# Two fused network layers on one core: Vector takes over some transposes, and the last tile is added and stored behind the branch that repeats the attention

## The chip, the cores and the metric

The kernel runs on one core of a Trainium2 chip. The metric is device time in microseconds (us). Three runs of the kernel before gave 2710.21, 2710.99 and 2712.02 us; the median is 2710.99 us. Engines are named as in the profile: PE is TensorE, with PEld its weight loads; DVE is VectorE, ACT is ScalarE, POOL is GpSimd, SP is the engine that issues every DMA here.

## The reference, cut to what matters

The input x is 2 x 56 x 56 x 384 (6272 tokens of 384 channels) in float32. Two layers follow one another.

```python
# layer 0
h = neighborhood_attention(layer_norm(x, ln1_g, ln1_b))   # 12 heads of 32, window 7 x 7
x = x + h                                                  # h: softmax(q k + rpb) v @ w_proj + b_proj
x = x + gelu(layer_norm(x, ln2_g, ln2_b) @ w1 + b1) @ w2 + b2
# layer 1
p = layer_norm(x, n1_g, n1_b) @ w_in + b_in                # 384 -> 768
local = depthwise_conv_3x3(p)
mixed = 0.25 * (ema_lr + ema_rl + ema_tb + ema_bt)(local) + local
x = x + layer_norm(mixed, on_g, on_b) @ w_out + b_out      # 768 -> 384
x = x + gelu(layer_norm(x, n2_g, n2_b) @ w1 + b1) @ w2 + b2
```

Both MLPs have 1536 hidden channels. The softmax is computed without subtracting a maximum; sums that leave the range 1e-9 to 1e9 set a flag, and a branch at the end repeats everything in a slower, safe way. With the inputs of this case the flag is not set.

## The kernel before, in words

Tokens lie in tiles of 128, 49 in all. The work is written out by hand in the order in which each engine gets it; an engine runs its instructions in that order, and so does the DMA queue of SP.

**Attention** (main loop of `block_kernel`, L702 to L806). There are 14 groups of 8 image rows, 4 windows of 8 x 14 queries in each, and 3 units of 4 heads in each window: 168 units, one a step `s`. A unit's scores go to two PSUM tiles (L515), DVE adds the bias (L530), ACT takes the exponent (L536). The keys of a window lie in 2 or 3 chunks. `gathered` (L538) adds the chunks of a unit on DVE, with one addition for 2 chunks and two for 3 (L542, L544). `values` (L546) multiplies each chunk with the values (L552) and the added numerators with ones (L558), which gives the sums for the softmax. `END` (L701) is 12: in the last two groups the planner has less left to put between the units.

**The step from attention to the rest.** At step `s == NU` (168) the keys' memory is freed, and SP is given the loads of the last four tiles' residuals (L741) and then those of the first two groups of the next stage (L742), all behind the stores of that step (`store_all`, L704). A residual gets its bias on POOL (`add_bias`, L569), either when its counter `loaded` runs out or when the projection's result is added (L583). After the loop the projections that are still open are added (L808, L585), then the first group is measured and normalized (L810 to L813), and the remaining projections follow.

**MLP of layer 0 and entry to layer 1** (`passes`, first loop, L1341 to L1404). 13 groups of 2, 3, and eleven times 4 tiles. For a group, `hidden` (L1053) is called 12 times (3 matmuls and one GELU), and `tokens` (L1059) once for each tile (12 matmuls). Beside that the group before is normalized (L1357), turned to channels and put through `project_in` (L1384), and the next group is normalized and turned (L1390). Turning is `channels` (L1038), which calls `to_channels` (L245): for each of 3 channel blocks one PE transpose a tile into PSUM (L251), and one ACT instruction that takes the block to SBUF with gain and bias (L254). The object `beside` hands out the convolution and the scans, nearly all on DVE, in small steps between those calls; its jobs begin when the first band of rows has been through `project_in`, in the fourth group.

**Exit of layer 1 and its MLP** (second loop, L1428 to L1455). 13 groups of 4 (eleven times), 3 and 2 tiles. `load_mix` (L1233) loads the mixed channels, `measure` (L1246) turns each tile with 6 PE transposes into PSUM (L1251) so that DVE can take mean and variance, and `project_out` (L1266) multiplies by `w_out`. `measure_beside` (L1257) calls `measure` after every second `hidden`; the group `half_way`, the seventh, is measured two calls of `hidden` later than the others, since its mixed rows are the last that the scans finish. In the `tokens` part of a group, the next group is normalized (L1450), turned by `channels` (L1442), and each finished tile is added and stored (L1447, L1448). PSUM tiles named `y` come from a pool of two (L967).

**The end.** After the last tile's addition and store, every engine loads the flag into a register (L1464) and branches on it (L1465) over the repeated attention, whose instructions fill a block as long as the main one; behind the branch lie only the waits and barriers that end the program.

Of the kernel before, what the change touches and what calls it, by code (L numbers as in the profile page):

```python
# [42 lines left out]
P = 128  # L43
# [130 lines left out]
def block_kernel(ctx: ExitStack, tc: tile.TileContext, ins: dict, out: bass.AP):  # L174
# [328 lines left out]
    class Unit:  # L503
# [34 lines left out]
        def gathered(self):  # L538

            n, t = self.w.keys, lp.tile([P, 4, TT], F32, name="sum", bufs=2)  # L540
            self.sum = t
            nc.vector.tensor_tensor(t[:n], self.pts[:n, :, 0, :], self.pts[:n, :, 1, :], ALU.add)  # L542
            for c in range(2, self.m):
                nc.vector.tensor_tensor(t[:n], t[:n], self.pts[:n, :, c, :], ALU.add)  # L544

        def values(self):  # L546

            w, hg, n = self.w, self.hg, self.w.keys
            for c in range(self.m):
                for i in range(4):  # L550
                    h = 4 * hg + i
                    nc.tensor.matmul(  # L552
                        o[i * HD : (i + 1) * HD, hg, :],
                        lhsT=w.vt[:n, c, h * HD : (h + 1) * HD], rhs=self.pts[:n, i, c, :],
                        start=c == 0, stop=c == self.m - 1,
                    )
            for i in range(4):
                nc.tensor.matmul(  # L558
                    sums[i * HD : (i + 1) * HD, hg * TT : (hg + 1) * TT], lhsT=ones_hd[:n, :],
                    rhs=self.sum[:n, i, :], start=True, stop=True,  # L560
                )

    def load_residual(t, pool=lp, bufs=3):

        xrs[t] = pool.tile([P, C], F32, name="xr", bufs=bufs)
        nc.sync.dma_start(out=xrs[t], in_=xf[t * P : (t + 1) * P, :])
        loaded[t] = 4

# [133 lines left out]
    for s in range(NU + 4):  # L702
        n, k, hg, i = s // UG, s % UG, s % NC, s // NC
        store_all()  # L704
        while load:
# [28 lines left out]
        if s >= NU - UG - 4 and hg == 2 and w_parts:  # L734
            w_parts.pop(0)()
        if s == NU:
            kctx.close()
            xp = ctx.enter_context(tc.tile_pool(name="x", bufs=2, side="right", reuse_waits="tile"))
            tail_pool = actx.enter_context(tc.tile_pool(name="a_tail", bufs=1))
            for t in range(T2 // P - 4, T2 // P):  # L740
                load_residual(t, tail_pool, 4)  # L741
            xs = {g: load_group(x1f, groups[g], "xa") for g in range(2)}  # L742


# [56 lines left out]
        if n + 3 < ng:  # L801
# [3 lines left out]
            if k in (8, 9, 11):  # L805
                taking.append(channels_of(n + 3, (8, 9, 11).index(k), turning_bank))  # L806

    for take in taking:  # L808
        take()
    norm = norm_of(xs[0], groups[0][1], sm)  # L810
    norm.close(groups[0][1])
    norm.shift(groups[0][1])
# [10 lines left out]
    actx.close()  # L823

    def attention_again():

# [4 lines left out]
        ps_t = fctx.enter_context(tc.tile_pool(name="f_pst", bufs=2, space=PSUM))  # L831
        ps_s = fctx.enter_context(tc.tile_pool(name="f_pss", bufs=4, space=PSUM))
        ps_o = fctx.enter_context(tc.tile_pool(name="f_pso", bufs=1, space=PSUM))
# [3 lines left out]
        nc.sync.dma_start(out=wproj, in_=ins["L0_conv_w_proj"].rearrange("(c p) n -> p c n", p=P))  # L837
        shift = fp.tile([P, C], F32, name="shift")
        nc.sync.dma_start(out=shift, in_=b_proj.to_broadcast([P, C]))
# [119 lines left out]

    def passes(xs, xn, w1, w2, between=lambda psum: None):  # L960
        pctx = ExitStack()
# [4 lines left out]
        cp = pctx.enter_context(tc.tile_pool(name="conv", bufs=2))  # L966
        ps_y = pctx.enter_context(tc.tile_pool(name="psy", bufs=2, space=PSUM))  # L967
        ps_t = pctx.enter_context(tc.tile_pool(name="pst", bufs=3, space=PSUM))
# [13 lines left out]

        rows = wp.tile([P, 2, C], F32, name="rows")
        w_in = wp.tile([P, NC, INNER], F32, name="w_in")
        w_out = wp.tile([P, NI, C], F32, name="w_out")

        def load_row(i, name):
            r = ROWS[name]
            nc.sync.dma_start(
                out=rows[:, i, :], in_=ins["rows"][r : r + 1, :].to_broadcast([P, C])  # L990
            )

        def row(name):
# [9 lines left out]
        def prepare_w_out():  # L1003
# [7 lines left out]
            nc.vector.tensor_scalar_mul(pair[:, :, 1], og, 1.0 / INNER)  # L1011
            ps = ps_y.tile([P, C], F32, name="y")
            for c in range(NI):
# [24 lines left out]
        def channels(xn, n, g, b):  # L1038
            hT = io.tile([P, NC, MT], F32, name="hT")
            to_channels(ps_t, [xn[:, k, :] for k in range(n)], hT, NC, g, b)  # L1040
            return hT

        def columns(w, m, hT, n):

            ps = ps_m.tile([P, MT], F32, name="mm")
            for c in range(NC):
                nc.tensor.matmul(  # L1047
                    ps[:, : n * P], lhsT=w[:, c, m * P : (m + 1) * P], rhs=hT[:, c, : n * P],
                    start=c == 0, stop=c == NC - 1,
                )  # L1050
            return ps
# [7 lines left out]
        def tokens(lhs, w, k):  # L1059

            ps = ps_y.tile([P, C], F32, name="y")
            for m, t in enumerate(lhs):
                nc.tensor.matmul(  # L1063
                    ps, lhsT=t[:, k * P : (k + 1) * P], rhs=w[:, m, :],
                    start=m == 0, stop=m == len(lhs) - 1,
                )
            return ps
# [165 lines left out]
        def load_mix(g):  # L1233
            t0, n = dgroups[g]
            mx = io.tile([P, NI, MT], F32, name="mx")
            for b, at, here, n in images(t0, n * P):
                nc.sync.dma_start(
                    out=mx[:, :, here : here + n],
                    in_=mix_d[b][:, :, at : at + n].rearrange("m p t -> p m t"),
                )  # L1240
            x = load_group(x2_d, dgroups[g], "xa")
# [14 lines left out]

        def measure_beside(m, g, ahead, late=0):  # L1257

            n = dgroups[g][1]
            k = (m - late) // 2 - 1  # L1260
            if m % 2 == 1 and 0 <= k < n:
                measure(ahead[0], ahead[2], k)
            if m == min(10 + late, NHID - 1):
                ahead[2].close(n)
# [72 lines left out]

        def channels_n1(xn, n):
            return channels(xn, n, "L1_conv_n1_g", "L1_conv_n1_b")

        for g, (t0, n) in enumerate(groups):  # L1341
            hid = []
            preparing = prepare_w_out() if g == 1 else iter(())
            if g == last:
# [3 lines left out]
            for m in range(NHID):  # L1348
                next(preparing, None)
                if waiting is not None:  # L1350
# [5 lines left out]
                    if 2 <= m < 2 + groups[gw][1]:  # L1356
                        norm_w.apply_by_scalar(m - 2, x2w, xn_w)  # L1357
                    if m == (11 if g == 1 else 6):
                        store_x2(gw, x2w)
                    if m == NHID - 1:  # L1360
                        hT_w = channels_n1(xn_w, groups[gw][1])
                hid.append(hidden(w1, m, hT, n, "L0_conv_b1"))
# [18 lines left out]
            if g == 0:  # L1381
                between(ps_y)
            if waiting is not None:
                project_in(gw, hT_w)  # L1384
            if g == last:
                w1, w2_1, w_parts = weights(1)
                for part in w_parts[:3]:
                    part()
            if g < last:
                hT = channels(xn_next, n_next, "L0_conv_ln2_g", "L0_conv_ln2_b")  # L1390
            x2 = io.tile([P, NT, C], F32, name="xc")
# [21 lines left out]
        x3, norm = project_out(0, *ahead)  # L1413
        hT = channels_n1(xn, groups[g][1])

# [10 lines left out]
        project_in(g, hT, first_input)  # L1426
        hT = channels(first["xn"], dgroups[0][1], "L1_conv_n2_g", "L1_conv_n2_b")
        for g, (t0, n) in enumerate(dgroups):  # L1428
            hid = []
            for m in range(NHID):  # L1430
                hid.append(hidden(w1, m, hT, n, "L1_conv_b1"))
                if g < last:
                    measure_beside(m, g + 1, ahead, 2 if g + 1 == half_way else 0)
                beside.go(MLP_D)
# [5 lines left out]
            for k in range(n):  # L1440
                if k == n - 1 and g < last:
                    hT = channels(xn, dgroups[g + 1][1], "L1_conv_n2_g", "L1_conv_n2_b")  # L1442
                ps = tokens(hid, w2, k)
                o = res[:, k, :]
                if k == 0 and g < last:
                    norm.shift(dgroups[g + 1][1])
                nc.vector.tensor_tensor(o, ps, o, ALU.add)  # L1447
                nc.sync.dma_start(out=yout[t0 + k * P : t0 + (k + 1) * P, :], in_=o)  # L1448
                if k == n - 3 and g < last:
                    xn = normalized(norm, x3, dgroups[g + 1][1])  # L1450
                    add_row(x3, dgroups[g + 1][1], "b2_1")
                beside.go(ROW_D)
# [4 lines left out]

    def raise_flag(psum):
        ps = psum.tile([P, C], F32, name="y")
        nc.tensor.matmul(ps[:1, :1], lhsT=bad, rhs=ones[:, :1], start=True, stop=True)  # L1460
# [4 lines left out]
    with tc.If(again > 0):  # L1465
# [5 lines left out]
        with tc.tile_pool(name="small_again", bufs=1) as sm_again:  # L1471
# [3 lines left out]
            xn = normalized(norm, xs[0], groups[0][1])  # L1475
        passes(xs, xn, w1, w2)


# [67 lines left out]
```

## Time and profile before

| what | value |
|---|---|
| median of three runs | 2710.99 us |
| the profiled execution, its own time | 2709.48 us |
| its span, first to last instruction | 2707.7 us |
| mean granted TensorE clock | 0.996 |
| ACT busy | 897.7 us, 33% |
| POOL busy | 249.6 us, 9% |
| DMA, mean over the span | 110 GB/s |
| PE transposes of normalized tiles, L251 | x441, 55.4 us, 275 ns each |
| PE transposes of mixed tiles, L1251 | x294, 40.8 us, 276 ns each |
| matmuls of the softmax sums, L558 | x1344, 259 ns each |

The span is cut into 40 slices in one part of the page, with the busy share of each engine in tenths. A group of instructions has its busy time, the mean duration of one, and the idle time of its engine just before it with what ended that. The program's float32 matmuls stand in the trace twice each (two passes), its transposes once. Durations of neighbouring PE instructions overlap, so a sequence is shorter than the sum of its durations.

### The profile page before, as it was taken

How to read it: one execution, taken by the hardware profiler on the slowest of the kernel's cores; microseconds unless marked ns; L12 is line 12 of the kernel's file. 1: busy time of each engine (PE TensorE's matmuls, PEld its weight loads, DVE VectorE, ACT ScalarE, POOL GpSimd, SP SyncE). 2: the span in 40 equal slices, each digit the busy share in tenths (PEclk: the TensorE clock that was granted, in tenths of full speed). 3: DMA queues.
4: the chain of work that ended last, by engine and by line, in shares of the span. 5: the costliest groups of instructions: out<-in, count | busy, mean ns of one | idle time of the engine just before them, and what ended most of it. 6: DMA issues, size and time to landing. Idle time of an engine off the chain costs nothing. (4 is left out here: it accounts for less than half of the span.)

```text
span 2707.7 us, 36333 instructions
## 1 busy us (share of the span) xinstructions
PE 2659.7 (98%) x14975; PEld 1492.9 (55%) x14975; DVE 1679.7 (62%) x2560; ACT 897.7 (33%) x1447; POOL 249.6 (9%) x264
## 2 busy tenths in 40 slices
PE   8999999998899999999999999999999999999998
PEld 4666666655555555555554555555555455555565
DVE  3778877878320188688989888898888522221110
ACT  4555555554222332222344422321233211111111
POOL 1111111111211100000010000000100011110100
PEclk9999999999999999999999999999999999999999
DMA  6423454225410132232354544443354411011000
GB/s 213 133 88 104 150 174 149 77 75 167 135 47 27 64 115 79 104 118 98 120 199 183 206 143 141 164 136 117 142 188 171 153 47 44 12 41 35 30 12 16
DMA packets 131887, 298.91 MB, mean 110 GB/s; under 512 B 10646, under 2 KB 87552, under 8 KB 129408
## 3 DMA queue, kind: packets, MB, share of 16 engines
q1 hardware_dynamic: 131712, 296.50, 31.9%
q8 instruction: 119, 1.95, 0.3%
q14 instruction: 56, 0.46, 0.1%
HBM read 180.86 MB, written 115.61 MB: 109 GB/s over the span
## 5 line engine op out<-in xcount | busy, mean ns | idle before, releaser
L1047 PE MATMUL mm<-hT,w 128*128 128x512 f32 (+2 forms) x1872 | 776.1, 570 | 0.1
L1063 PE MATMUL y<-w,hid 128*128 128x384 f32 x2352 | 764.8, 486 | 0.0
L1063 PEld LDWEIGHTS y<-w,hid 128*128 128x128 f32 x2352 | 445.0, 190 | 305.3 <-issue 0.5
L1047 PEld LDWEIGHTS mm<-hT,w 128*128 128x128 f32 x1872 | 352.1, 191 | 372.8 <-issue 342.4
L1056 ACT ACTIVATE hid<-mm,chan 128x512 f32<-128x512 f32 (+2 forms) x312 | 206.3, 662 | 741.2 <-PE mm L1047 741.2
L1141 DVE SCALAR_TENSOR_TENSOR loc<-pt,taps,loc 128x990 f32<-128x990 f32 (+9 forms) x336 | 377.1, 1122 | 10.0 <-ACT loc L1123 1.7
L536 ACT ACTIVATE pts<-pts 119x448 f32<-119x448 f32 (+3 forms) x336 | 206.5, 642 | 187.9 <-DVE pts L530 187.9
L530 DVE TENSOR_TENSOR pts<-sc,bias 119x448 f32<-119x448 f32 (+3 forms) x336 | 220.8, 699 | 67.7 <-PE sc L515 66.7
L222 POOL TENSOR_TENSOR rs<-rs,mhalf 128x4 f32<-128x4 f32 (+4 forms) x67 | 87.2, 1302 | 1745.6 <-DVE rs L219 1704.1
L386 PE MATMUL ps<-hT,wqkv 128*128 128x448 f32 x504 | 211.9, 559 | 3.5 <-ACT vs L431 1.5
L1047 PE MATMUL mm<-hT,w_in 128*128 128x512 f32 (+2 forms) x468 | 191.7, 568 | 0.6 <-ACT hT L254 0.6
L1063 PE MATMUL y<-w_out,mx 128*128 128x384 f32 x588 | 191.8, 486 | 0.0
L1395 DVE TENSOR_TENSOR xc<-y,xa 128x384 f32<-128x384 f32 x49 | 27.3, 557 | 251.0 <-PE y L1063 250.5
L1447 DVE TENSOR_TENSOR xc<-y,xc 128x384 f32<-128x384 f32 x49 | 27.2, 555 | 218.2 <-PE y L1063 167.8
L1063 PEld LDWEIGHTS y<-w_out,mx 128*128 128x128 f32 x588 | 111.6, 190 | 79.8 <-issue 4.8
L240 ACT ACTIVATE xn<-xc,sh,rs 128x384 f32<-128x384 f32 x98 | 64.7, 698 | 269.3 <-DVE sh L233 269.1
L214 DVE BATCH_NORM_STATS2 st<-xi 128x6 f32<-128x384 f32 x98 | 50.3, 554 | 153.3 <-PE xi L1251 153.2
L1047 PEld LDWEIGHTS mm<-hT,w_in 128*128 128x128 f32 x468 | 88.7, 190 | 101.6 <-issue 91.8
L386 PEld LDWEIGHTS ps<-hT,wqkv 128*128 128x128 f32 x504 | 90.2, 191 | 84.4 <-issue 72.8
L254 ACT ACTIVATE hT<-tp,chan 128x512 f32<-128x512 f32 (+2 forms) x117 | 79.5, 751 | 165.1 <-PE tp L251 165.0
L515 PEld LDWEIGHTS sc<-qT,kT 32*100 32x100 f32 (+3 forms) x3168 | 90.9, 169 | 69.5 <-DVE pts L530 17.3
L515 PE MATMUL sc<-qT,kT 32*100 32x112 f32 (+3 forms) x3168 | 113.8, 270 | 9.0 <-DVE pts L530 8.4
(89 smaller groups left out, 2435.4 us busy)
## 6 DMA issues: line engine op xcount, KB each, us to landing
bias<-in_bias_t SPq DMA_DIRECT2D x16, 1344.0 KB
loc<-loc_d SPq DMA_DIRECT2D x24, 784.0 KB
mixed<-mix_d SPq DMA_DIRECT2D x24, 784.0 KB
mix_d<-mixed SPq DMA_DIRECT2D x24, 784.0 KB
xa<-x_d SPq DMA_DIRECT2D x22, 768.0 KB
p_d<-mx SPq DMA_DIRECT2D x10, 1536.0 KB
mx<-mix_d SPq DMA_DIRECT2D x10, 1536.0 KB
pt<-p_d SPq DMA_DIRECT2D x18, 560.0 KB
```

The lines of the kernel that those rows point to most:

```text
L214: nc.vector.bn_stats(st[:n, i, :], x)
L222: nc.gpsimd.tensor_tensor(rs, rs, mhalf[:n, :k], ALU.pow)
L240: nc.scalar.activation(out[:, k, :], x[:, k, :], AF.Identity, bias=self.sh[:n, k : k + 1], scale=self.rs[:n, k : k + 1],)
L254: nc.scalar.activation(dst[:, c, : len(xs) * n], tp, AF.Identity, bias=col(b, c), scale=col(g, c))
L386: nc.tensor.matmul(ps, lhsT=wqkv[:, c, m * P : (m + 1) * P], rhs=hT[:, c, half_of(n)], start=c == 0, stop=c == NC - 1,)
L515: nc.tensor.matmul(sc[i // 2][: w.keys, i % 2, (first + c) * TT : (first + c + 1) * TT], lhsT=kT[d, hg, w.keys_at + r * w.kc : w.keys_at + ...
L530: nc.vector.tensor_tensor(self.of(half), sc[half][:n, :, at].rearrange("p h (c q) -> p h c q", q=TT), self.w.bias[:n, 4 * self.hg + h : 4 ...
L536: nc.scalar.activation(self.of(half), self.of(half), AF.Exp)
L1047: nc.tensor.matmul(ps[:, : n * P], lhsT=w[:, c, m * P : (m + 1) * P], rhs=hT[:, c, : n * P], start=c == 0, stop=c == NC - 1,)
L1056: nc.scalar.activation(t[:, : n * P], ps[:, : n * P], AF.Gelu, bias=col(b1, m))
L1063: nc.tensor.matmul(ps, lhsT=t[:, k * P : (k + 1) * P], rhs=w[:, m, :], start=m == 0, stop=m == len(lhs) - 1,)
L1141: nc.vector.scalar_tensor_tensor(to, pt[:, lo + dy - self.top : hi + dy - self.top, xt : xt + n], self.tap(dy, dx), to, ALU.mult, ALU.add,)
```

## The change

It has seven parts.

1. In the last two attention groups DVE no longer adds the chunks; PE multiplies every chunk with ones and accumulates.
2. At step 168 the loads of the next stage's first groups are issued first, ahead of that step's stores, and the last residuals get their bias two steps later rather than at the end; the first group is measured before the open projections are added.
3. In the first loop of `passes`, from the second group until the scans begin, the turning is done by DVE in blocks of 32 x 32, and ACT applies gain and bias in SBUF.
4. In the second loop, from `half_way` on, the turning of the next group is done in the same way, its normalization is moved up to the first tile, and the tiles after `half_way` are measured from blocks that DVE turned.
5. The group `half_way` is loaded in steps of 128 tokens and measured at the same calls of `hidden` as the others.
6. One of the two PSUM tiles `y` becomes `y_end`, which outlives `passes`; the calls take the two in turn.
7. The last tile's residual is copied to `rows`; its addition to `y_end` and its store stand behind the branch.

```diff
         def gathered(self):
-            n, t = self.w.keys, lp.tile([P, 4, TT], F32, name="sum", bufs=2)
-            self.sum = t
+            n, self.parts = self.w.keys, [self.pts[:, :, c, :] for c in range(self.m)]
+            if self.w.n >= END:
+                return
+            t = lp.tile([P, 4, TT], F32, name="sum", bufs=2)
+            self.parts = [t]
...
-            for i in range(4):
-                nc.tensor.matmul(
-                    sums[i * HD : (i + 1) * HD, hg * TT : (hg + 1) * TT], lhsT=ones_hd[:n, :],
-                    rhs=self.sum[:n, i, :], start=True, stop=True,
-                )
+            for c, part in enumerate(self.parts):
+                for i in range(4):
+                    nc.tensor.matmul(
+                        sums[i * HD : (i + 1) * HD, hg * TT : (hg + 1) * TT], lhsT=ones_hd[:n, :],
+                        rhs=part[:n, i, :], start=c == 0, stop=c == len(self.parts) - 1,
+                    )
...
+        if s == NU:
+            kctx.close()
+            xp = ctx.enter_context(tc.tile_pool(name="x", bufs=2, side="right", reuse_waits="tile"))
+            tail_pool = actx.enter_context(tc.tile_pool(name="a_tail", bufs=1))
+            xs = {g: load_group(x1f, groups[g], "xa") for g in range(2)}
+            for t in range(T2 // P - 4, T2 // P):
+                load_residual(t, tail_pool, 4, 2)
         store_all()
...
-            for t in range(T2 // P - 4, T2 // P):
-                load_residual(t, tail_pool, 4)
-            xs = {g: load_group(x1f, groups[g], "xa") for g in range(2)}
...
+    norm = norm_of(xs[0], groups[0][1], sm)
+    norm.close(groups[0][1])
     for take in taking:
         take()
-    norm = norm_of(xs[0], groups[0][1], sm)
-    norm.close(groups[0][1])
     norm.shift(groups[0][1])
...
+        def turned(xn, k, hT):
+            for i in range(0, P, HD):
+                for j in range(0, P, HD):
+                    nc.vector.transpose(
+                        hT[j : j + HD, :, k * P + i : k * P + i + HD],
+                        xn[i : i + HD, k, :].rearrange("p (c q) -> p c q", c=NC)[:, :, j : j + HD],
+                    )
+        def scaled(hT, n, g, b):
+            for c in range(NC):
+                nc.scalar.activation(
+                    hT[:, c, : n * P], hT[:, c, : n * P], AF.Identity, bias=col(b, c),
+                    scale=col(g, c),
+                )
...
+            step = P if g == half_way else n * P
...
+        def measure_by_vector(mx, norm, k):
+            t = flat(half("turned", "work"))[:, : NI * P]
+            for i in range(0, P, HD):
+                for j in range(0, P, HD):
+                    nc.vector.transpose(
+                        t[j : j + HD].rearrange("p (m c) -> p m c", m=NI)[:, :, i : i + HD],
+                        mx[i : i + HD, :, k * P + j : k * P + j + HD],
+                    )
+            norm.add(k, [t[:, h * C : (h + 1) * C] for h in range(2)])
...
+            if g > half_way:
+                if m % 2 == 0 and m // 2 < n:
+                    measure_by_vector(ahead[0], ahead[2], m // 2)
+            elif m % 2 == 1 and 0 < m // 2 <= n:
+                measure(ahead[0], ahead[2], m // 2 - 1)
+            if m == 10:
                 ahead[2].close(n)
...
+            by_vector = 0 < g < last and not beside.busy()
...
+                    if by_vector and 3 <= m < 3 + groups[gw][1]:
+                        turned(xn_w, m - 3, hT_w)
...
+            if by_vector:
+                hT = io.tile([P, NC, MT], F32, name="hT")
+                for k in range(n_next):
+                    turned(xn_next, k, hT)
+                scaled(hT, n_next, *ln2)
...
+            by_vector = half_way <= g < last
...
+                if by_vector and 0 < k < n - 1:
+                    for q in range(2 * k - 2, min(2 * k, dgroups[g + 1][1])):
+                        turned(xn, q, hT)
+                elif by_vector and k == n - 1:
+                    scaled(hT, dgroups[g + 1][1], *n2)
...
+                if g == last and k == n - 1:
+                    assert ps is y_end and t0 + n * P == T2
+                    nc.vector.tensor_copy(rows[:, 1, :], o)
+                    break
                 nc.vector.tensor_tensor(o, ps, o, ALU.add)
...
         passes(xs, xn, w1, w2)
+    o = rows[:, 1, :]
+    nc.vector.tensor_tensor(o, y_end, o, ALU.add)
+    nc.sync.dma_start(out=yout[T2 - P :, :], in_=o)
```

## The prediction

> **What bounds the kernel now.** I read the busy shares first, then the waits of PE, then stretches of single stages.
>
> ```profile
> PE 2659.7 (98%) x14975; PEld 1492.9 (55%) x14975; DVE 1679.7 (62%) x2560; ACT 897.7 (33%) x1447; POOL 249.6 (9%) x264
> ...
> DVE  3778877878320188688989888898888522221110
> ```
>
> PE is busy for 98% of the span. DVE (one digit for each fortieth) is nearly idle in two places: around slices 11 to 13, before the scans begin, and from slice 31 to the end. What PE waits for, with total, times and longest, in us:
>
> ```profile
> PE sc L515 <- DVE pts L530: 8.4, 15, 1.5
> PE tp L251 <- DVE bad L820: 7.4, 1, 7.4
> PE xi L1251 <- DMA mx<-mix_d: 4.8, 1, 4.8
> ```
>
> Stretches (start:end, length, then PE, PEld, DVE, ACT, POOL busy, granted clock, DMA): one group of the second loop, the last two attention groups, and PE's restart after its 7.4 us wait.
>
> ```profile
> 2211.40:2292.70 81.30, 81.30 (x253) 44.74 (x252) 16.33 (x31) 12.86 (x19) 8.85 (x4) 1.00 0.12 39
> 616.00:652.00 36.00, 33.38 (x570) 21.23 (x562) 32.05 (x66) 17.41 (x30) 2.86 (x8) 1.00 0.47 157
> 652.00:687.00 35.00, 25.75 (x512) 16.98 (x512) 30.00 (x66) 14.37 (x29) 7.58 (x13) 1.00 0.67 209
> 708.20:713.60 5.40, 5.40 (x16) 4.40 (x17) 3.34 (x11) 3.23 (x5) 0.00 (x0) 0.50 0.85 174
> ```
>
> In the second loop PE has no gap and DVE works 16.3 us of 81.3: what leaves PE there shortens the time. In the attention's last groups PE is idle 2.6 and 9.3 us. After the long wait PE runs at half clock for 5.4 us.
>
> **1. Transposes leave PE.** In the first loop 21 tiles are turned by DVE (2+3+4 for layer 1, 4+4+4 for the next group), in the second 21 (4+4+4+4+3+2), with 3 PE transposes each: 126. The same last 21 tiles are measured by DVE, 6 each: 126. So 252 go. In order of time, two sequences:
>
> ```profile
> 2283.70 1.47 PE L251 MATMUL tp<-ident,xn 128*128 128x128 f32 x12
> ...
> 2303.06 0.82 PE L1251 MATMUL xi<-ident,mx 128*128 128x128 f32 x6
> ```
>
> One lasts 0.273 us, so they follow at (1.47 - 0.273)/11 = 0.109 us, and (0.82 - 0.273)/5 = 0.109. 252 x 0.109 = **27.5 us**, all on PE's unbroken path.
>
> What covers it is DVE's idleness. DVE gets 16 transposes a tile: 32x96 elements for turning, 32x192 for measuring. The trace has no such form. Rows, by form:
>
> ```profile
> L498 DVE STREAM_TRANSPOSE rec_t<-wide 128x352 f32<-128x352 f32 x56 | 30.0, 536 | 3.1 <-POOL wide L494 3.1
> ...
> L219 DVE SCALAR_TENSOR_TENSOR rs<-mv,ones 128x4 f32<-128x4 f32 x44 | 6.9, 157 | 0.9
> ```
>
> The bounds are 0.16 us (an instruction with next to no elements) and 0.54 us (one that moves more). A line through both gives 0.157 + 92 x 1.09 ns = 0.26 us for 96 elements and 0.36 for 192, and I take these, one after another without overlap. Measuring a tile: 16 x 0.36 + two statistics at 0.56 + 0.21 = 7.1 us, four tiles 28.4 us, begun when a group begins. PE spends 12 x 2.58 = 31 us in `hidden`, then 3.87 us on each tile of `project_out`, and has two banks: it needs the result (after 1.0 us on POOL) only at 38.7 us. Turning: from the end of the group's first `tokens` call DVE has an addition (0.6), 32 transposes (8.3), an addition, 32 transposes: 17.8 us, then 0.7 us on ACT; PE comes for it after three calls of 12 x 2 x 0.3225 = 7.74 us, at 23.2. In the first loop there is more room, 31 us of `tokens` behind each. So no stall, cost nothing; the cover of turning ends when 64t + 1.9 = 23.2, at t = 0.33 us.
>
> The page VectorE: DVE Perf Modes of the Trainium skill, section Two Vector instructions with no wait between them, speaks against the change. Rows first: two bias additions of 0.614 us in a row (L530) start 0.53 apart, so 0.08 us of each is hidden. The rule: an instruction whose output starts in another group of 32 partitions than the last output waits until all earlier ones have ended, and here every transpose writes another group than the one before. By the row a turning transpose would cost 0.18 us, by the rule 0.26; neither reaches 0.33, so the sum is the same by both, but by the rule the margin is a fifth.
>
> **2. Sums on PE.** 30 additions at 0.62 us leave DVE (18.6 us); 120 matmuls, 240 in the trace, come to PE. In the timeline, going from 16 to 24 matmuls of the same shape on L552 adds 0.19 us (0.59 to 0.78), so 30 x 0.19 = 5.7 us: 18 of the 30 in group 12, where PE has 2.6 us of idleness to give back (loss 3.4 - 2.6 = 0.8), and 12 in group 13, where 2.3 us meet 9.3 us of idleness, mostly behind DVE's bias additions. If a bit over half of that idleness goes, 5 - 2.3 = 2.7. Net **-2 us**; ends +5.7 (nothing was DVE's) and -6.2 (all idleness goes: 5.7 - 11.9).
>
> **3. Attention to MLP.** PE waited 7.4 us for the last projection additions (L585), which waited for four bias additions on POOL (0.96 us apart), which stood behind the norm's power, which waited for `xa`: issued 695.6 us, landed 701.15, behind five residual loads that were held until 693.33. Now `xa` stands behind no store, can issue near 688.4, after the weights of 687.9. But SP's order now puts a store and the one remaining residual load behind all of these: 2.7 MB from 687.9 at the 217 GB/s of that stretch is 12.5 us, so that residual lands near 701 to 702, and POOL's addition, one DVE addition, the shift and four more additions (about 4 us) end near 705 to 706 where it was 708.1. I take **-3 us**, with the half clock kept. Ends: nothing; and 7.4 + 2.7 (half of 5.4 us) = -10.
>
> **4. The half-way group.** PE waited 4.8 us at its sixth `hidden` (2139.3 to 2144.1) for the whole load of 448 tokens. In the changed kernel it arrives after four, 5.2 us earlier, at 2134.1 of the old clock. The first tile is two small loads: the first one landed at 2139.96, and the second, issued at 2135.6 after a scan's store had landed, should follow in about as long as 196 KB took, 1.2 us: 2141.2. PE then has two `hidden` more to do than before: 2141.2 + 5.2 = 2146.4 against 2144.1, **+2.3 us**. The scans end when DVE ends them; DVE waits for PE 9.8 us in the 135 us up to there and over 40 in the 250 before 1250, so it moves with PE's earlier start. Ends: -2 (the tile lands 4 us sooner) and +6 (more half clock).
>
> **5. The end.** Register loads and branches of the engines (duration in ns, start):
>
> ```profile
> L1465 PEldq COMPARE_BRANCH  x1: 3607/3607/3607, 2695.0 to 2695.0; - x1
> ...
> L1465 DVEq COMPARE_BRANCH  x1: 72/72/72, 2701.1 to 2701.1; - x1
> L1465 SPq COMPARE_BRANCH  x1: 50/50/50, 2702.3 to 2702.3; - x1
> L1465 DVEq EVENT_SEMAPHORE  x1: 21/21/21, 2704.6 to 2704.6; - x1
> ...
> L1465 SPq EVENT_SEMAPHORE  x8: 17/17/17, 2705.0 to 2705.5; - x8
> ```
>
> PE's last matmul ends at 2700.4; DVE adds to 2701.03, SP issues the store at 2701.06, and it lands by 2704.18. DVE and SP branch after that, and their next instruction comes 3.4 and 2.6 us later, so SP begins its closing waits at 2705.0 and the span ends at 2707.64. PE's branch lay under its matmuls. Behind the branch, DVE and SP branch from about 2694 and are through by 2698, inside the 7.2 us that DVE waits for the last tile. The addition adds a wait for PE's own step behind the branch (0.05 us); the store lands near 2704.3, eight waits of 0.065 follow instead of sixteen: 2704.9 where the old one stood at 2706.1. **-1.6 us** with part of the closing fetch still to pay; ends 0 and -2.5. The copy of the residual lies in DVE's wait. Part 6 keeps two banks in turn and costs nothing.
>
> **Sum.** -27.5 - 2 - 3 + 2.3 - 1.6 = -31.8 us. The profiled execution took 2709.48 (span 2707.7 and 1.8 outside it), so 2677.7; it lay 1.5 us under the median of the runs. I predict 2678.
>
> **Rivals.**
> - *The small gains come in full.* Transition -10, sums -6, the tile lands early -2, end -2.5: 27.5 + 20.5 = 48 less, 2661. For it: all the idleness is in the waits. Against it: DMA is at 0.57 to 0.85 busy around 690, and the vt loads hold PE 3.4 us in group 13.
> - *They cost instead.* Sums +5.7, half-way +6, transition and end 0: 2709.5 - 27.5 + 11.7 = 2694. For it: PE is short of idleness in group 12.
> - *DVE becomes the bound*, the other side. If a 32-partition transpose costs 0.54 us whatever its size, turning takes 1.9 + 64 x 0.54 = 36.5 us against 23.2, 13.3 us a group, in four groups with some 3 us more from measuring, 8 in the two small ones, and some 23 in the first loop, where the layer-1 input is late: 65 + 8 + 23 = 96, so about 2774. It turns slower than before from the point where stalls eat 31.8 us, near t = 0.43. Against: a full-width transpose of 352 elements costs 0.54.
> - *Vector turns, yet PE waits a little* (t = 0.36 to 0.40, 2 to 4 us in five groups): about 2692, inside the range.
>
> **Numbers.** Forecast 0.62 (2668 to 2688), gains in full 0.12, costs or short waits 0.17, DVE the bound 0.09, of which 0.07 end slower. The range for 8 in 10 goes from 2664 to 2697. A change of 0.2%, 5.4 us, is about what a measurement of this kernel can tell from none: faster 0.91, same 0.02, slower 0.07.
>
> **What would show it.** Right: 315 transposes on L251's successor and 168 on L1251's, no wait of PE for `hT` from ACT in groups seven to twelve, a 32x96 transpose at 0.2 to 0.3 us, PE's wait at the half-way group near 7 us, DVE's and SP's branches before the last matmul. Wrong: PE waits for `scaled` or for banks held by DVE; the first passes' transposes still wait 7 us; the span ending over 6 us after the last matmul.

## The result and the profile after

| | before | after |
|---|---|---|
| median of the runs shown | 2711.15 us (4 runs, 2710.21 to 2712.02) | 2678.78 us (4 runs, 2677.15 to 2682.41) |
| ratio, with its 95% interval | | 0.9882 [0.9867, 0.9897] |
| the profiled execution, its own time | 2709.48 us | 2680.04 us |

The forecast was 2678. The first two rows to compare are busy time and the slices of DVE, from the page of the changed kernel:

```profile
PE 2640.3 (99%) x14963; PEld 1473.9 (55%) x14963; DVE 1963.2 (73%) x3539; ACT 898.7 (34%) x1447; POOL 249.7 (9%) x264
...
DVE  3778877876365698688989889888988627677652
```

PE lost 19 us of busy time and DVE took on 284 us: its two idle places are filled (2, 0, 1 became 6, 5, 6 in slices 12 to 14, and 2, 2, 2, 1, 1, 1 became 7, 6, 7, 7, 6, 5 in slices 34 to 39). PE's waits, in the same form as before (total, times, longest):

```profile
PE xi L1288 <- DMA mx<-mix_d: 7.7, 1, 7.7
...
PE ps L582 <- DVE xr L590: 3.6, 2, 2.6
...
PE tp L251 <- DVE bad L825: 0.7, 1, 0.7
```

The wait of 7.4 us ahead of the first passes' transposes is gone; 3.6 us of it now lie at the last projections. The wait at the half-way group grew from 4.8 to 7.7 us. To see what each stage gained, I cut both traces at PE's own landmarks: first scores, last scores, start of the second `hidden` group, start of the half-way stage (`hidden` beside which that group is measured), start of the next group, last matmul. Columns are start:end, length, PE, PEld, DVE, ACT, POOL busy, granted clock, DMA share and GB/s. The kernel before, then the changed one:

```profile
48.46:682.85 634.39, 617.56 (x8706) 379.05 (x8706) 502.78 (x1038) 338.59 (x621) 89.75 (x163) 1.00 0.38 125
682.85:743.87 61.02, 52.02 (x263) 36.02 (x256) 16.98 (x46) 14.84 (x27) 13.28 (x14) 0.92 0.44 138
743.87:2123.70 1379.83, 1379.09 (x4096) 733.19 (x4095) 1037.56 (x1225) 431.26 (x619) 86.07 (x50) 1.00 0.36 128
2123.70:2211.47 87.77, 82.94 (x253) 45.58 (x252) 24.93 (x39) 12.86 (x19) 12.27 (x5) 0.98 0.24 82
2211.47:2700.37 488.90, 488.90 (x1546) 276.83 (x1544) 85.06 (x169) 78.86 (x123) 43.91 (x23) 1.00 0.09 31
```

```profile
46.31:685.75 639.44, 626.61 (x8923) 387.65 (x8922) 487.86 (x1010) 338.63 (x621) 90.26 (x163) 0.99 0.38 125
685.75:741.20 55.45, 50.54 (x287) 34.45 (x280) 14.75 (x44) 14.88 (x27) 12.88 (x13) 1.00 0.44 145
741.20:2114.40 1373.20, 1372.47 (x4034) 726.34 (x4033) 1126.39 (x1560) 431.64 (x619) 86.05 (x50) 1.00 0.36 129
2114.40:2205.70 91.30, 83.64 (x253) 45.86 (x252) 25.38 (x41) 12.86 (x19) 12.28 (x5) 0.96 0.25 78
2205.70:2673.90 468.20, 468.20 (x1357) 257.45 (x1355) 296.37 (x842) 79.48 (x123) 43.94 (x23) 1.00 0.10 33
```

With the start (48.46 to 46.31) and the end (7.3 to 4.3 us behind the last matmul) this splits the difference of the spans, 29.5 us: start -2.2, attention +5.0, step to the MLP -5.6, first loop -6.6, half-way stage +3.5, rest of the second loop -20.7, end -3.0. In the two loops PE has next to no gap in either kernel (0.7 us in the first loop, none in the second), and there the shortening is the transposes alone. The start cannot be the change's, since the instructions up to the first scores are the same. Whether the +5.0 is the change's was the first question for the experiments.

### The profile page after: what moved, and what is told of

The parts are those of the page before. It is cut to its first block, busy times and chain, and to the rows that moved or that the text cites. A ratio compares the mean times of both kernels' runs of the same rounds, so it can differ in the third digit from the quotient of the medians.

```text
span 2678.2 us, 37275 instructions
## 1 busy us (share of the span) xinstructions
PE 2640.3 (99%) x14963; PEld 1473.9 (55%) x14963; DVE 1963.2 (73%) x3539; ACT 898.7 (34%) x1447; POOL 249.7 (9%) x264
## 5 line engine op out<-in xcount | busy, mean ns | idle before, releaser
L1096 PE MATMUL y_end<-w,hid 128*128 128x384 f32 x1200 | 395.2, 486 | 0.0
L1096 PE MATMUL y<-w,hid 128*128 128x384 f32 x1152 | 379.4, 486 | 0.0
L1096 PEld LDWEIGHTS y_end<-w,hid 128*128 128x128 f32 x1200 | 227.5, 190 | 157.2
L1096 PEld LDWEIGHTS y<-w,hid 128*128 128x128 f32 x1152 | 218.2, 190 | 150.5 <-issue 1.0
L1064 DVE STREAM_TRANSPOSE hT<-xn 32x96 f32<-32x96 f32 x672 | 181.1, 269 | 31.4 <-PE mm L1080 11.8
L1299 DVE STREAM_TRANSPOSE turned<-mx 32x192 f32<-32x192 f32 x336 | 123.3, 367 | 4.2
L556 PE MATMUL o<-pts,vt 100*32 100x112 f32 (+3 forms) x3168 | 112.7, 266 | 3.8 <-DMA vt<-v_d 2.7
L582 PE MATMUL ps<-wproj,og 128*128 128x384 f32 x294 | 107.1, 503 | 3.6 <-DVE xr L590 3.6
```

What stands on the lines that cost most here:

```text
L556: nc.tensor.matmul(o[i * HD : (i + 1) * HD, hg, :], lhsT=w.vt[:n, c, h * HD : (h + 1) * HD], rhs=self.pts[:n, i, c, :], start=c == 0, stop ...
L582: nc.tensor.matmul(ps, lhsT=ogs[t // 7][:, c, at : at + P], rhs=wproj[:, c, :], start=c == 0, stop=c == NC - 1,)
L1064: nc.vector.transpose(hT[j : j + HD, :, k * P + i : k * P + i + HD], xn[i : i + HD, k, :].rearrange("p (c q) -> p c q", c=NC)[:, :, j : j ...
L1096: nc.tensor.matmul(ps, lhsT=t[:, k * P : (k + 1) * P], rhs=w[:, m, :], start=m == 0, stop=m == len(lhs) - 1,)
L1299: nc.vector.transpose(t[j : j + HD].rearrange("p (m c) -> p m c", m=NI)[:, :, i : i + HD], mx[i : i + HD, :, k * P + j : k * P + j + HD],)
```

## The experiments

All kernels are the changed one with one edit, unless said otherwise. Ratios are to the kernel before, run beside each.

**1. `sums_on_vector`: part 1 undone.**

```diff
-            if self.w.n >= END:
+            if self.w.n >= ng:
```

> The changed kernel without its part 1: DVE adds the chunks in all groups. The trace of the changed kernel has the last scores 5.0 us later than before once the different start (2.2 us) is taken out, where the prediction had 2 us earlier. Theory: the 240 matmuls and the half clock that their gaps brought cost PE time there; without them the last scores come 3.5 to 5 us earlier, and since the residual loads behind follow the attention's end, the run is 2 to 4 us shorter than the 2678.8 of the changed kernel: 2675 to 2677. Rival: the late scores cost nothing, because the last projections wait for the residuals' loads anyhow: 2678 to 2679, with a longer wait of PE ahead of the first passes' transposes.

Measured: 2680.76 us (2678.86 to 2682.71), ratio 0.9892 [0.9875, 0.9908]. The theory falls: without PE's additional matmuls the run is not shorter. The rival's longer wait ahead of the first passes' transposes does not show either (0.7 us, as in the changed kernel). The trace says why the first reading misled: the attention stage took 639.8 us with the very code that took 634.4 us in the trace of before.

**2. `sums_only`: the kernel before with part 1 alone**, and second traces of both kernels, unchanged.

> The kernel before with part 1 alone: in the last two attention groups PE multiplies all chunks with ones and DVE adds none. Theory after the run with the sums on DVE (2.0 us slower than the changed kernel, and as long in the attention as it): part 1 is worth nothing that can be told, from 2 us faster to 2 us slower than before, and the 5 us between the two first traces came from stretches at half clock that fall differently in every execution. Rival, as the two first traces read: PE's additional matmuls cost 5 us here, and the run is 3 to 5 us slower than before.

> The kernel before, unchanged, for a second trace. From the first to the last scores its first trace took 634.4 us with 3.4 us at half clock, where the same attention code took 639.8 us with 17.1 us at half clock in the run with the sums on DVE. Theory: the stretches at half clock depend on how the short waits fall on the clock's own raster of 3.41 us, and this trace lies anywhere between the two, with a time that follows the half-clock stretches at about 0.4 us for each us. Rival: 634 us again, and the difference belongs to an edit.

> The changed kernel, unchanged, for a second trace. Theory: transposes, transition, half-way group and end differ from the first trace by less than 1 us each, and the start (up to 2.5 us) and the attention's last groups (up to 5 us) by more. Rival: all stages repeat within 0.5 us.

Measured: `sums_only` 2712.42 us (11 runs, 2710.78 to 2715.97), ratio 1.0007 [0.9998, 1.0016]; the second executions took 2710.69 and 2682.31 us. Stages in us, with the time at half clock (granted clock 0.50) inside the first two:

| trace | sums | start | attention (half clock) | step to MLP (half clock) | first loop | half-way | second loop | end |
|---|---|---|---|---|---|---|---|---|
| before | DVE | 48.46 | 634.39 (3.4) | 61.02 (10.2) | 1379.83 | 87.77 | 488.89 | 7.31 |
| before_again | DVE | 46.91 | 636.31 (6.8) | 60.59 (10.2) | 1379.82 | 89.24 | 488.89 | 7.12 |
| sums_on_vector | DVE | 48.89 | 639.85 (17.1) | 52.32 (0) | 1373.19 | 91.65 | 468.19 | 4.34 |
| sums_only | PE | 47.40 | 635.19 (6.8) | 62.81 (10.2) | 1379.81 | 87.89 | 488.89 | 7.12 |
| after | PE | 46.31 | 639.44 (13.7) | 55.46 (0) | 1373.19 | 91.31 | 468.19 | 4.34 |
| after_again | PE | 47.73 | 637.62 (10.2) | 57.94 (6.8) | 1373.18 | 91.42 | 468.19 | 4.34 |

The two loops and the end repeat to a few hundredths, but for the kernel before's end. The start moves by 2.5 us and the attention by 5 us between executions of the same code, and the attention follows its half-clock time: 5.46 us more for 13.7 us more at half clock among the three with the sums on DVE, 0.40 for each. By this reading, which rests on three traces, most of the attention's +5.0 in the first pair is how PE's short gaps fell, and not the change. Part 1 is worth nothing that these runs can tell: by medians 1.5 us slower alone (from 0.5 faster to 4.3 slower), 2 us faster inside the changed kernel, less than the spread of its runs. One expectation fell: the step to the MLP was to repeat within 1 us in the changed kernel's second trace, and it moved by 2.5 us, with 6.8 us at half clock that the first trace did not have.

**3. `old_transition`: part 2 undone.**

```diff
-            xs = {g: load_group(x1f, groups[g], "xa") for g in range(2)}
-            for t in range(T2 // P - 4, T2 // P):
-                load_residual(t, tail_pool, 4, 2)
         store_all()
...
+            for t in range(T2 // P - 4, T2 // P):
+                load_residual(t, tail_pool, 4)
+            xs = {g: load_group(x1f, groups[g], "xa") for g in range(2)}
...
-    norm = norm_of(xs[0], groups[0][1], sm)
-    norm.close(groups[0][1])
     for take in taking:
         take()
+    norm = norm_of(xs[0], groups[0][1], sm)
+    norm.close(groups[0][1])
```

> The changed kernel without its part 2: the stores of step 168 and the residual loads stand ahead of the first groups' loads again. Theory: PE gets its 7 us wait back, and with it a stretch of some 5 us at half clock, which together are worth 5.6 us by the two traces (3.6 up to the first hidden block, 1.9 after it): 2684.4. The prediction's term of 3 us would give 2681.8. Rival: the shorter wait came from part 1, whose later scores hide the loads, and not from the order of the loads: 2679 to 2680.

Measured: 2684.77 us (2683.40 to 2686.67), ratio 0.9904 [0.9888, 0.9921], so 6.0 us more than the changed kernel; the step to the MLP took 63.0 us. The theory holds (5.6). The wait is back, in the words of the waits of PE:

```profile
PE tp L251 <- DVE bad L824: 7.6, 1, 7.6
```

and behind it 10.2 us at half clock, as in the kernel before. In the changed kernel's first trace the clock is full from 706 to 714 us, where before 708.2 to 713.6 stood at 0.50:

```profile
706.00:714.00 8.00, 7.04 (x34) 5.28 (x33) 4.18 (x14) 4.35 (x8) 0.47 (x1) 1.00 0.78 233
```

In its second trace 6.8 us at half clock begin at 705.8, behind a wait of only 2.1 us at the last projections; so the long wait always goes, the half clock only in some executions. Over all traces the step takes 52.3 to 58.3 us in the ten with part 2 and 60.6 to 63.0 in the four without.

**4. `tail_inside`: part 7 undone.**

```diff
-                if g == last and k == n - 1:
...
-                    nc.vector.tensor_copy(rows[:, 1, :], o)
-                    break
                 nc.vector.tensor_tensor(o, ps, o, ALU.add)
...
-    o = rows[:, 1, :]
-    nc.vector.tensor_tensor(o, y_end, o, ALU.add)
-    nc.sync.dma_start(out=yout[T2 - P :, :], in_=o)
```

> The changed kernel without its part 7: the last tile is added and stored ahead of the branch. By the two traces the stretch from the last matmul to the end went from 7.3 to 4.3 us, so theory: 3.0 us longer, 2681.8. The prediction's term of 1.6 us would give 2680.4. Rival: part of the 3.0 us was chance in how the closing code is fetched, and the run is longer by 1 us or less: under 2680.

Measured: 2685.99 us (2683.37 to 2686.92), ratio 0.9908 [0.9892, 0.9925]. The end took 7.93 us where the changed kernel's takes 4.34 in both its traces, so part 7 is worth 2.8 to 3.6 us by the ends (with part 7 the end takes 4.34 us in nine traces of ten, 3.57 in the other). The time itself is 7.2 us longer, more than the theory's 3.0. In this kernel's trace the rest lies ahead of the edit: the attention took 641.8 us, with waits of 7.0 us for the `vt` loads (2.7 in the changed kernel). I have no cause for that in the edit.

**5. `turning_on_tensor`: parts 3 and 4 undone.**

```diff
-            by_vector = 0 < g < last and not beside.busy()
+            by_vector = False
...
-            by_vector = half_way <= g < last
+            by_vector = False
...
-            if g > half_way:
+            if g > last:
```

> The changed kernel without its parts 3 and 4: all tiles are turned and measured by PE transposes, as in the kernel before. Theory: 252 transposes of 0.109 us come back to PE's unbroken path, 27.4 us, and nothing else moves: 2678.8 + 27.4 = 2706.2, with the second loop's period back at 81.3 us from 77.3. Rival: DVE's new work also delays the additions and statistics that others wait for, so that the transposes are worth more than the step showed and taking them back gives part of it away: under 2703.

Measured: 2709.21 us (11 runs, 2704.45 to 2712.89), ratio 0.9993 [0.9984, 1.0002]. So nearly the whole gain is in these two parts; the other five together give 1.9 us (from 4.3 faster to 0.5 slower). By medians the transposes are worth 30.4 us, by the stages 6.6 + 20.7 = 27.3; the stages are the sharper measure, since they leave out the attention, and they are the theory's figure. Nothing speaks for the rival.

The single worths do not add up to that 1.9 us: undoing part 2 cost 6.0 us and the ends give part 7 some 3 us, while part 5 costs 2 to 3, which leaves 6 to 7 us. In the traces the gap lies in the attention. From the first scores to the second `hidden` group, attention and step together, the kernel before took 695.4 and 696.9 us, the changed one 694.9 and 695.6, this run 695.0: most of what the step gains the attention ahead of it loses. On average over all traces the step is 5.5 us shorter in those with part 2 and the attention 2.8 us longer. Why it is longer stays open: part 2 comes behind the last scores in the program.

**6. `turned_twice`: how wide the cover is.**

```diff
-            for i in range(0, P, HD):
+            for i in [*range(0, P, HD)] * 2:
                 for j in range(0, P, HD):
                     nc.vector.transpose(
```

> The changed kernel with every tile that DVE turns turned twice over (the second time with the same result); measuring is unchanged. The changed kernel shows 0.283 us from one turning transpose to the next, 18.6 us for four tiles, and the scaled result 1.7 us before PE needs it. Theory (the cover as the prediction reckoned it): four groups of the second loop wait 18.6 - 1.7 = 16.9 us each, the group of three tiles 14.0 - 6.8 = 7.2, that of two 4.5, so 79 us; in the first loop the layer-1 inputs of the second and third group come late by some 8 and 17 us: about 104 us in all, 2783. Rival: the cover is wider than that, since PE's queue still holds token blocks and DVE's other work can wait: under 2740.

Measured: 2864.37 us (2862.39 and 2866.34), ratio 1.0565 [1.0546, 1.0584]: 186 us more, not 104. In the second loop the theory holds: 93 us in all against 79, since transposes now follow at 0.300 us; four groups lose 17 to 20 each, about half of it right ahead of the next `hidden`. The first loop lost 87 instead of 25. PE's timeline shows two kinds of wait (start, length, what, idle before it with its releaser):

```profile
824.09 9.42 PE L1096 MATMUL y_end<-w,hid 128*128 128x384 f32 x24 [24.34 <-DVE xc L1458]
```

```profile
2389.35 33.31 PE L1080 MATMUL mm<-hT,w 128*128 128x512 f32 x72 [10.24 <-ACT hT L1071]
```

The first is the one I had not seen. DVE's timeline at that place:

```profile
785.04 38.41 DVE L1064 STREAM_TRANSPOSE hT<-xn 32x96 f32<-32x96 f32 x128
823.48 0.56 DVE L1458 TENSOR_TENSOR xc<-y_end,xa 128x384 f32<-128x384 f32 x1
```

The addition that frees the PSUM tile stands behind 128 transposes in DVE's order, and PE with two `y` tiles runs dry long before it needs the turned result. In the changed kernel the same addition starts at 788.43, for a tile that PE finished near 786, and PE needs its bank back at 793.5: the cover there was 4.5 us, not the 31 us of token blocks.

PE idles 70 us in the first loop and 68 in the second; the rest of the loss goes with 82 and 72 us at half clock, which the changed kernel's loops do not have. Of the 70 us, 40 are waits for such additions and 26 are of a third kind, for a GELU on ACT: in ACT's order a normalization stands ahead of it, which needs a value from DVE (L233), and DVE computes that only behind the transposes of other tiles (in one group behind 64 of them, 19.2 us, at 871.8).

**7. `order_of_blocks`: does the output's place slow a transpose?**

```diff
-            for i in range(0, P, HD):
-                for j in range(0, P, HD):
+            for j in range(0, P, HD):
+                for i in range(0, P, HD):
```

> The changed kernel with the two loops of the turning exchanged, so that four transposes in a row write the same 32 partitions and only every fourth goes to another group. [...] If the spacing does not depend on the output's partitions, it stays at 0.283 us and 18.1 us. The time is the changed kernel's by both, since turning is covered.

Measured: 2679.58 us (one run), inside the range of the changed kernel's runs. DVE's timeline of one group's turning:

```profile
2337.39 9.03 DVE L1064 STREAM_TRANSPOSE hT<-xn 32x96 f32<-32x96 f32 x32
2346.45 0.56 DVE L1525 TENSOR_TENSOR xc<-y_end,xc 128x384 f32<-128x384 f32 x1
2346.92 9.03 DVE L1064 STREAM_TRANSPOSE hT<-xn 32x96 f32<-32x96 f32 x32
```

32 transposes take 9.03 us in either order, 0.283 from one to the next, and each follows the last 0.013 us behind its end. This does not speak against the rule that the prediction names. By the Trainium skill (VectorE: DVE Perf Modes, Two Vector instructions with no wait between them) an instruction is held until all earlier ones have ended when its output or an input starts in another group of 32 partitions than the last one in the same memory did. With the loops exchanged the output keeps its group for four transposes, but the input then changes its group with every one, so every transpose is held in both orders, and equal spacing is what the rule gives. The third line agrees with it: the first transpose of that set reads and writes the same group as the addition ahead of it, and it begins at 2346.92, 0.09 us before that addition ends at 2347.01. So do the first transposes of all eleven sets that follow an addition directly, by 0.08 to 0.09 us. Whether two transposes in a row with both groups unchanged would overlap, no run here shows.

**8. The half-way group: `half_way_whole`, `split_and_later`, `half_way_latest`.** The first loads it in one piece and measures it two calls of `hidden` later than the others; the second keeps the split load and measures two calls later; the third measures after calls 6, 8, 10 and 11, counted from zero, where the changed kernel measures after calls 3, 5, 7 and 9.

```diff
-            step = P if g == half_way else n * P
+            step = n * P
```

```diff
+            late = 2 if g == half_way else 0
...
-            elif m % 2 == 1 and 0 < m // 2 <= n:
-                measure(ahead[0], ahead[2], m // 2 - 1)
-            if m == 10:
+            elif m % 2 == 1 and 0 < (m - late) // 2 <= n:
+                measure(ahead[0], ahead[2], (m - late) // 2 - 1)
+            if m == min(10 + late, NHID - 1):
```

```diff
+            elif g == half_way:
+                if m in (6, 8, 10, 11):
+                    measure(ahead[0], ahead[2], (6, 8, 10, 11).index(m))
...
-            if m == 10:
+            if m == (11 if g == half_way else 10):
```

> The changed kernel without its part 5: the half-way group is loaded in one piece of 448 and 64 tokens and measured two hidden blocks later than the other groups. Theory: the group's data come when the scans end, in one piece some 2.5 us later than the first 128 tokens did; PE arrives at about 2130.0 instead of 2124.6 and waits some 4.8 us instead of 7.7, and the run is about 3 us shorter: 2675.5. Rival: the split load is what brings the data in time, and its loss costs as much as the later place gives: 2678 to 2680.

> The changed kernel with the half-way group still loaded in steps of 128 tokens but measured two hidden blocks later, as the kernel before did. Theory: the first 128 tokens are there at 2132.3 as before, and PE comes for them at 2129.8 instead of 2124.6, so the wait of 7.7 us shrinks to some 2.5 and one of the two half-clock stretches behind it may go: 5 to 6.5 us less than the changed kernel, 2672.5 to 2674, and 2 to 3 us less than with the whole load. Rival: the later tiles or the later close of the norm then keep PE waiting at the projection, and the gain over the whole load is nothing: 2676.

> The changed kernel with the half-way group's four tiles measured after the seventh, ninth, eleventh and twelfth hidden blocks instead of the second, fourth, sixth and eighth calls of the others; the split load stays. Two blocks later had left a wait of 2.2 us. Theory: the first 128 tokens are there before PE comes, the wait goes, and the run is about 2 us under the 2674.2 of two blocks later: 2672. Rival: the last tile's statistics come too late for the projection's two banks, and PE waits there instead: 2674 or more.

| kernel | load | first measured after call | PE's wait, us | half-way stage, us | median, us | ratio |
|---|---|---|---|---|---|---|
| after | split | 3 | 7.7 | 91.3 | 2678.78 | 0.9882 [0.9867, 0.9897] |
| half_way_whole | whole | 5 | 4.9 | 89.3 | 2676.22 | 0.9872 [0.9856, 0.9889] |
| split_and_later | split | 5 | 2.2 | 83.6 | 2674.24 | 0.9865 [0.9850, 0.9880] |
| half_way_latest | split | 6 | none | 81.3 | 2670.78 | 0.9854 [0.9839, 0.9869] |

By the waits and the stages all three theories hold; by the medians the second gained 4.5 us where 5 to 6.5 were expected, and the third 3.5 more where 2 were. The split brings the first tile 2.4 us sooner (2132.5 against 2135.5, the latter in a trace whose stage starts 0.7 us later), and the earlier call throws that away. PE's timeline of the second, then the half-way stage of the third, which has PE busy throughout at full clock:

```profile
2134.43 0.84 PE L1288 MATMUL xi<-ident,mx 128*128 128x128 f32 x6 [2.15 <-DMA mx<-mix_d]
```

```profile
2114.98:2196.26 81.28, 81.28 (x253) 44.75 (x252) 24.79 (x39) 12.86 (x19) 12.30 (x5) 1.00 0.28 88
```

`half_way_latest` beats both kernels: 8.0 us below the changed one, 40 below the one before.

## Why the prediction came out

The total was 0.8 us off, but that flatters its small terms: their errors cancel.

| step | forecast, us | first pair of traces, us | what the runs say |
|---|---|---|---|
| transposes leave PE | -27.5 | -27.3 | held, in every trace |
| sums on PE | -2 | +5.0 (attention) | nothing that can be told; -2 not confirmed |
| attention to MLP | -3 | -5.6 | 2.7 by the second pair, 6.0 when undone |
| half-way group | +2.3 | +3.5 | 2.2 by the second pair, 2.6 for part 5 undone |
| the end | -1.6 | -3.0 | 2.8 to 3.6 |
| start | none | -2.2 | chance |

- **Transposes.** 0.109 us each was the right price because PE had no gap around them; the instruction counts are those forecast (315 on L251, 168 on L1288). The line through two rows gave 0.26 and 0.36 us for DVE's two shapes; the page of the changed kernel has

```profile
L1064 DVE STREAM_TRANSPOSE hT<-xn 32x96 f32<-32x96 f32 x672 | 181.1, 269 | 31.4 <-PE mm L1080 11.8
...
L1299 DVE STREAM_TRANSPOSE turned<-mx 32x192 f32<-32x192 f32 x336 | 123.3, 367 | 4.2
```

- **The cover.** ACT's and PE's timelines show what is left of it in the second loop: the scaled result is ready at 2281.3, PE starts on it at 2283.0.

```profile
2279.10 2.22 ACT L1071 ACTIVATE hT<-hT,chan 128x512 f32<-128x512 f32 x3 [18.09 <-DVE hT L1064]
```

```profile
2283.04 27.20 PE L1080 MATMUL mm<-hT,w 128*128 128x512 f32 x63
```

  1.7 us over 64 transposes is 0.027 each, so it ends near 0.31 us and not at 0.33: the forecast had 0.7 us for ACT, which works through three blocks in 2.2. In the first loop the forecast named the wrong cover (run 6); it cost nothing only because DVE was fast enough. The rival with DVE as the bound is real, and its 96 us at 0.54 was likely too small for that reason: it had 23 us for the first loop, which lost 87 in run 6, with two transposes of 0.300 us for each block.
- **Sums.** The step that failed. It took PE's idle time in one trace as a fixed stock to be given back. That idleness, and the half clock behind it, differs by 5 us between executions of the same code.
- **Attention to MLP.** The wait went as forecast. The size lay between two executions: I kept the half clock, and it was gone in the first trace (-5.6) and there in the second (-2.7, close to the -3), although the long wait was gone in both. What the forecast left out is that the attention ahead of the step took longer, so that the two together gained 0.5 us in the first pair and 1.3 in the second, where -2 and -3 were forecast. The residual behind the store did hold the last projections, as forecast: PE's transposes began at 707.7, close to 708.2, but with projections instead of a 7 us gap ahead of them.
- **Half-way group.** Right in place and size: PE came at 2124.9, which is 2134.2 by the old clock (the changed kernel's stage starts 9.3 us earlier), against 2134.1 forecast, and the first tile let it go at 2132.5, or 2141.8, against 2141.2.
- **The end.** Too small by 1.4 us. DVE and SP branch ahead of the last matmul, as forecast:

```profile
L1543 DVEq COMPARE_BRANCH  x1: 72/72/72, 2666.9 to 2666.9; - x1
L1543 SPq COMPARE_BRANCH  x1: 50/50/50, 2668.1 to 2668.1; - x1
...
L1543 DVEq EVENT_SEMAPHORE  x1: 21/21/21, 2670.3 to 2670.3; - x1
```

```profile
2674.08 0.56 DVE rows L1556
```

  The second fence is the last piece of the chain that ended last: the addition starts 0.2 us behind the last matmul's end at 2673.9, so nothing of the branch stands in its way. The forecast left the last store at its old 3.1 us and kept part of the gap ahead of the last barrier. The store, issued at 2674.67, had landed by 2676.52, and the gap of 1.2 us that the old trace has ahead of the last barrier was gone.

## What to carry to other kernels

Work moved to an idle engine is free only as long as nothing that the busy engine waits for stands behind it in the idle engine's order: look for the additions that free a bank first, and only then for the moved work's own deadline. A load cut into smaller pieces pays only if its user is also moved to where the first piece arrives; here the piece came 2.4 us sooner and its user 5.2. Idle time of a few us in one trace is no stock to be earned: cut several traces at the same landmarks and take only what repeats.

## What the hardware showed that I had not expected

- Every full stretch at half clock ahead of the end is a multiple of 3.41 us long (3.41, 6.83, 10.24, 13.65, 23.89), and within a trace they start whole multiples apart (583.87, 655.55, 679.44, 2130.11 in the changed kernel). Whether a gap of 1 to 2.5 us brings one differed between executions: a gap of 1.35 us at 652.3 in the changed kernel was followed by 3.4 us at half clock, one of 1.47 at 651.6 in the kernel before by none. The same attention code took 634.4 to 639.8 us, longer with more time at half clock.
- Transposes in blocks of 32 partitions take 269 ns for 96 elements and 367 ns for 192 on average and do not overlap: those of 96 elements followed each other at 0.283 us in both orders of the blocks. This agrees with the Trainium skill (VectorE: DVE Perf Modes, Two Vector instructions with no wait between them), since in both orders each transpose changes the group of 32 partitions that it reads, writes, or both.
